# Attention's pair sums two steps behind their additions, and the scan's products with C in pairs of steps

## The chip, the cores and the metric

The kernel runs on one core of a Trainium2 chip, written in Bass with Tile. A core has five engines that work through queues of their own: PE (TensorE: matrix products, weights loaded by PEld), DVE (VectorE), ACT (ScalarE), POOL (GpSimd) and SP (SyncE, which here issues DMAs). SBUF holds 128 partitions; PSUM has 8 banks of 2 KB per partition, and products land there. The metric is the device time of one execution in microseconds, lower is better. Before the change it is 2339.04 us, the median of four runs from 2338.34 to 2341.28.

## The reference

One layer: x is 4 images of 256 channels and 32 × 32 pixels (N = 1024 tokens). A mixer with a residual is followed by a mixture of experts with a residual. The part that the change touches:

```python
def selective_scan(u, dt, Bm, Cm, A, Dp):          # per channel, 16 states
    dA = jnp.exp(dt[..., None] * A)
    dBu = (dt * u)[..., None] * Bm[:, :, None, :]
    def step(h, inp):
        dA_t, dBu_t, C_t = inp
        h = dA_t * h + dBu_t
        return (h, jnp.einsum('bds,bs->bd', h, C_t))
    ...
    return ys + u * Dp
def mamba(xs, ...):                                # 4 of them, 64 channels each, inner width 128
    u, z = jnp.split(xs @ inw.T, 2, axis=-1)
    u = silu(causal_conv(u)); xdbc = u @ xpw.T
    dt = softplus(xdbc[..., :4] @ dtw.T + dtb)
    return selective_scan(...) * silu(z) @ outw.T
def mha(x, ...):                                   # 8 heads of 32
    att = softmax(q @ k.T / hd ** 0.5)
    return (att @ v) @ outw.T + outb
...
xm = mamba_v(layernorm(xs)) + skip_scale * xc      # then gates and convolutions along the tokens
x_local = conv1d(xm2); x_global = mha(xm2)
x_out = gelu(layernorm(concat([x_local, x_global]) @ fc_w.T + fc_b))
...                                                # 3x3 convolution, layernorm, projection
```

After it come the experts: 8 of them, 256 to 1024 to 256 with gelu, the two best for each token, weighted.

## The kernel before

Every engine's queue holds its instructions in the order in which the code emits them; the scheduler moves nothing. Buffers are rotating slots of pools: `act8` (8 KB a partition, 8 slots), `act4` (4 KB, 7 slots), `act2` (2 KB, 17 slots), and `ps`, the 8 PSUM banks. An instruction that writes a slot waits until the slot's last reader is done.

*The scan.* For image b and channel quarter n (inner width 128) a tile holds 32 channels × 4 states on its partitions and half of the tokens (512) on its free axis. A part (b, n, h) is half h of the tokens; it has 16 steps i, with q, g = divmod(i, 4): block q of four states, channel group g of 32. One step is: `decay`, dA = exp(dt·A) on ACT, emitted three steps ahead (L620); `inflow`, dBu on DVE into a PSUM bank (L628); `step`, the recurrence as one DVE scan instruction (L639), then for h = 0 a POOL copy of the last column, from which h = 1 goes on (L643), and on POOL the product of the states with C (L644, `hs` by `cs`). Once a block, `sums_of` lets PE add the four states of each channel: four products with the constant `quads` into the bank `yp` (L650). `spread_b` makes the block's B with PE (`bs`, L612), `spread_c` its C by four DMAs from SP (`cs`). The function `scan` emits, in this order, step i of a part: at g = 1 `spread_b` of the next block; entries of the table `before` (the end of the part before: last sums, `gather`, `project_out`, `add_skip`); of `behind` (dt of the next part: `dtp`, softplus, two POOL products L575 and L579, `dts` by DMA); of `group` (projections of the next quarter: `project_z`, `project_u` at 9 and 10 with product `up` L528, `silu`, which reads them into u at L549, `project_c`); `spread_c` at g = 0; at g = 1 `sums_of` of the block before; then decay, inflow and step. `gather` is DVE's y (L657) and POOL's product with z (L660); `project_out` is PE's `op` (L665); `add_skip` writes `xm` on DVE (L671).

*Around it.* While image b is scanned, the convolutions of image b−1 run between the steps (`depthwise3`, products `fp`, gate g; their first product is `qd`, L802, which reads xm once the image is whole). In the middle of the image the scan stops, the attention of b−1 runs, with the three-by-three taps of b−2 (L1161) and the layernorm of b+1 (`normalised`, L472) beside it, and the scan goes on when attention is almost over; `joined` then does the fc product of b−1. After the last image come its convolutions, its attention, and 35 tiles of expert work.

*Attention.* 32 steps (g, h, kt) per image: two groups of four heads, two halves of the queries, eight tiles of 128 keys. A step emits the logits of the next step (PE `st`, four banks, L967; ACT's four exps, L977), then values times exps (PE into the values bank, L1013). Softmax's denominators: at odd kt DVE adds the four exps of kt to those of kt−1 (L1023), and at the next step, ahead of that step's other work on DVE, `sum_pair` lets PE add them over the keys (L987; the profile writes its output as `av`). Both banks, values and sums, are taken at kt = 0. A block (g, h) ends in `end_block` at the next block's kt = 1, after its adds: ACT's Ln and Exp (L995, L1000), DVE's reduce (L999) and multiply (L1003).

Of the kernel before, what the change touches and what calls it, by code (L numbers as in the profile page):

```python
# [9 lines left out]
F32 = mybir.dt.float32  # L10
AF = mybir.ActivationFunctionType
ALU = mybir.AluOpType
AX = mybir.AxisListType

P = 128
# [4 lines left out]
HALF = 512  # L20
NB, DM, DIN, DS, DTR, KC = 4, 64, 128, 16, 4, 4
NHEAD, HD = 8, 32
# [50 lines left out]
def network(  # L73
# [27 lines left out]
    nc = tc.nc  # L101
# [41 lines left out]

    with tc.tile_pool(name="w_conv", bufs=1) as wp, tc.tile_pool(
        name="act8", bufs=8
    ) as act8, tc.tile_pool(name="act4", bufs=7) as act4, tc.tile_pool(
        name="act2", bufs=17
    ) as act2, tc.tile_pool(name="steps", bufs=2) as actd, tc.tile_pool(
        name="steps4", bufs=6
    ) as acts, tc.tile_pool(name="rows", bufs=3) as actc, tc.tile_pool(  # L150
        name="small", bufs=1
    ) as small, tc.tile_pool(
        name="spread", bufs=2, space=bass.MemoryType.DRAM
# [123 lines left out]
        ones = experts.every  # L277


        GD, GS = DIN // 32, DS // 4  # L280
# [58 lines left out]
        def ps(name):  # L339

            return psum.tile([P, HALF], F32, tag="ps", name=name)
# [9 lines left out]

        def a4(name):
            return act4.tile([P, N], F32, tag="a4", name=name)

        def a2(name, rows=P):
            return act2.tile([rows, HALF], F32, tag="a2", name=name)

        def half(h):
            return ts(h, HALF)
# [3 lines left out]
        def log_exp():  # L363
            if loaded[0] != LOG_EXP:
                nc.scalar.preload_act_table_set(LOG_EXP)
                loaded[0] = LOG_EXP
# [150 lines left out]
        T = {}  # L517
# [90 lines left out]
        def spread_b(b, n, h, q):  # L608
            bs = T[b, n, h, "bs", q] = ps(f"bs_{b}_{n}_{h}_{q}")
            for i, r in enumerate(states):  # L610
                s = DTR + 4 * q + i
                nc.tensor.matmul(  # L612
                    bs[r], xpwT_s[:, n, s : s + 1].to_broadcast([P, 32]),
                    T[b, n, "u"][:, half(h)], start=True, stop=True,
                )
# [16 lines left out]
        def step(b, n, h, i):  # L632
            q, g = divmod(i, GD)
            dBu = T.pop((b, n, h, "dBu", i))
            hs = T[b, n, h, "hs", i] = a2(f"hs_{b}_{n}_{h}_{i}")
            if h == 0 and i == 0:
                T[b, n, "last"] = small.tile([P, NSTEP], F32, tag="last", name=f"last_{b}_{n}", bufs=2)
            last = T[b, n, "last"][:, i : i + 1]
            nc.vector.tensor_tensor_scan(  # L639
                hs, T[b, n, h, "dA", i], dBu, 0.0 if h == 0 else last, ALU.mult, ALU.add  # L640
            )
            if h == 0:
                nc.gpsimd.tensor_copy(last, hs[:, HALF - 1 : HALF])  # L643
            nc.gpsimd.tensor_tensor(hs, hs, T[b, n, h, "cs", q], ALU.mult)  # L644

        def sums_of(b, n, h, q):
            if q == 0:
# [19 lines left out]
        def add_skip(b, n, h):  # L667
# [7 lines left out]


        before = {
            1: [(sums_of, GS - 1)], 3: [(gather,)], 6: [(project_out,)], 8: [(add_skip,)],
        }

        behind = {
# [44 lines left out]
        def scan(at, i, stop):  # L726

            b, n, h = parts[at]
            q, g = divmod(i, GD)
            if g == 1 and q + 1 < GS:  # L730
                spread_b(b, n, h, q + 1)
            if at > 0:
                for what, *args in before.get(i, ()):
                    if parts[at - 1] not in finished:
                        what(*parts[at - 1], *args)
            if at + 1 < len(parts):
                for what, *args in behind.get(i, ()):
                    if what is not spread_b or not stop:
                        what(*parts[at + 1], *args)
            nb, nn = (b, n + 1) if n + 1 < NB else (b + 1, 0)  # L740
            if nb < B:
                for what, *args in group[h].get(i, ()):
                    what(nb, nn, *args)
            if g == 0 and q + 1 < GS:
                spread_c(b, n, h, q + 1)
            if g == 1 and q > 0:
                sums_of(b, n, h, q - 1)
            ahead = i + LEAD
            if ahead < NSTEP:
                decay(b, n, h, ahead)  # L750
            elif at + 1 < len(parts) and not stop:
                decay(*parts[at + 1], ahead - NSTEP)
            if i + 1 < NSTEP:
                inflow(b, n, h, i + 1)
            elif at + 1 < len(parts) and not stop:
                inflow(*parts[at + 1], 0)
            step(b, n, h, i)

        finished = set()
# [149 lines left out]
        NK = N // P  # L909
# [38 lines left out]
        def attention(b):  # L948

            v8, qk = QKV.pop(b)
            rows = [
                largest(b, g, qk[g][:, 0, :], qk[g][:, 1, :]) if shifted else None
                for g in range(2)
            ]
            yield 1
            steps = [(g, h, kt) for g in range(2) for h in range(2) for kt in range(NK)]

            def logits(g, h, kt):

                q, k = qk[g][:, 0, :], qk[g][:, 1, :]
                sts = [ps(f"st_{b}_{g}_{h}_{kt}_{i}") for i in range(4)]
                for i in range(4):
                    r = ts(i, HD)
                    nc.tensor.matmul(  # L967
                        sts[i], k[r, ts(kt, P)], q[r, half(h)], start=True, stop=not shifted
                    )
                    if shifted:  # L970
                        nc.tensor.matmul(
                            sts[i], ones[HD * i : HD * i + 1, :],
                            rows[g][HD * i : HD * i + 1, half(h)], start=False, stop=True,
                        )
                es = [a2(f"e_{b}_{g}_{h}_{kt}_{i}") for i in range(4)]
                for i in range(4):
                    nc.scalar.activation(es[i], sts[i], AF.Exp, scale=1.0 / HD**0.5)  # L977
                return es

            log_exp()  # L980
            ahead = logits(*steps[0])
            pairs, accs, ending = [], [None, None], []

            def sum_pair():
                kt, acc, es = pairs.pop()
                for i in range(4):
                    nc.tensor.matmul(  # L987
                        acc[ts(i, HD)], ones[:, 0:HD], es[i], start=(kt == 1), stop=(kt == NK - 1)
                    )

            def end_block(g, h, values, total):

                low, out = a2(f"low_{b}_{g}_{h}"), OT[b][g][:, half(h)]
                at = (2 * b + g) * 2 + h
                nc.scalar.activation(low, total, AF.Ln, bias=added)  # L995
                if shifted:
                    nc.scalar.activation(low, low, AF.Exp, scale=-1.0)
                else:
                    nc.vector.tensor_reduce(sums[:, 0, at : at + 1], total, AX.X, ALU.max)  # L999
                    nc.scalar.activation(  # L1000
                        low, low, AF.Exp, scale=-1.0, accum_out=sums[:, 1, at : at + 1]
                    )
                nc.vector.tensor_tensor(out, values, low, ALU.mult)  # L1003

            for at, (g, h, kt) in enumerate(steps):
                es = ahead
                if at + 1 < len(steps):
                    ahead = logits(*steps[at + 1])
                if kt == 0:

                    accs = [ps(f"av_{b}_{g}_{h}_{w}") for w in range(2)]
                for i in range(4):
                    nc.tensor.matmul(  # L1013
                        accs[0][ts(i, HD)], v8[:, kt, ts(4 * g + i, HD)], es[i],
                        start=(kt == 0), stop=(kt == NK - 1),
                    )
                if pairs:
                    sum_pair()
                if kt % 2 == 0:
                    first = es  # L1020
                else:
                    for i in range(4):
                        nc.vector.tensor_tensor(first[i], first[i], es[i], ALU.add)  # L1023
                    pairs.append((kt, accs[1], first))
                    if ending:
                        end_block(*ending.pop())
                if kt == NK - 1:
                    ending.append((g, h, *accs))
                if at == len(steps) - 3:
                    T["attended", b] = True  # L1030
                yield 1
            sum_pair()
            yield 1
            end_block(*ending.pop())
            yield 1

        def local(b):
# [317 lines left out]
        with tc.manual_schedule(engines=ALL):  # L1355
# [4 lines left out]
            for b in range(B):  # L1360
                for p in range(PARTS):
                    at = b * PARTS + p
                    stop = b > 0 and p == PARTS // 2 - 1 or at == len(parts) - 1
# [71 lines left out]
class Experts:  # L1435
# [11 lines left out]
    T = 256  # L1447
# [649 lines left out]
```

## Time and profile before

| | |
|---|---|
| median of four runs | 2339.04 us (2338.34 to 2341.28) |
| profiled execution | 2339.41 us, of which 2337.6 us are the span |
| mean granted PE clock | 0.928 |
| PE, DVE, ACT, POOL busy | 2040.3, 1608.9, 1145.3, 1111.6 us |
| L644, product with C, 512 times | 673.4 us, mean 1318 ns (1257 to 2302) |
| L643, copy of the last column, 256 times | 61.8 us, mean 241 ns |
| L639, scan, 384 rows found | 475.2 us, mean 1268 and 1207 ns |
| attention of images 0 to 3 | 472 to 571, 858 to 958, 1292 to 1392, 1730 to 1820 us |
| experts | about 1850 to 2337 us |

The profile is of one execution of the program. Times are microseconds unless marked ns. "L644" is line 644 of the kernel. In the rows of single instructions the first two columns are the start from the beginning of the span and the duration; x8 says how many instructions are drawn together; what stands in square brackets is idle time of the engine ahead of the row, and the instruction whose end was waited for. In rows of groups, the figures after the first bar are the busy time in us and the mean ns of one, after the second the idle time ahead of them and what ended it. A few per cent of the product rows are missing from the record.

### The profile page before, as it was taken

The numbers are of one execution on the slowest core, as the hardware profiler recorded it, in microseconds if no ns is written. First come the engines' busy times: TensorE is split into PE (matmuls) and PEld (weight loads), VectorE is DVE, ScalarE is ACT, GpSimd is POOL, SyncE is SP. The second block draws the span as 40 slices with busy tenths as digits, with TensorE's granted clock in tenths as the row PEclk, the third lists the DMA queues.
The fourth block names the chain that finished last, engine by engine and source line by source line (L and its number), as shares of the span: only waits on it lengthen the run. The fifth ranks groups of instructions, "written<-read, shape, count | busy, mean of one in ns | idle before, by whom it ended". The sixth has DMA issues, their size and how long they took to land. (4 is left out here: it accounts for less than half of the span.)

```text
span 2337.6 us, 28285 instructions
## 1 busy us (share of the span) xinstructions
PE 2040.3 (87%) x8810; PEld 917.0 (39%) x8810; DVE 1608.9 (69%) x2295; ACT 1145.3 (49%) x1953; POOL 1111.6 (48%) x1185
## 2 busy tenths in 40 slices
PE   7777776999976899986669999668999999999995
PEld 2122111332211232222113223205752678888884
DVE  3989998967898989789989877987355264211111
ACT  3654546468656467664264775415258432222221
POOL 0788887722787750476877115572140012422221
PEclk7987988999998999998789999768999999999997
DMA  2454443310343330133433202443340165877765
GB/s 85 122 143 111 110 107 78 81 38 29 95 103 93 83 73 28 44 102 96 120 76 74 55 1 59 104 136 117 86 139 1 43 193 171 256 196 194 195 186 156
DMA packets 155022, 244.33 MB, mean 105 GB/s; under 512 B 34212, under 2 KB 103492, under 8 KB 154856
## 3 DMA queue, kind: packets, MB, share of 16 engines
q1 hardware_dynamic: 135680, 217.07, 33.6%
q0 software_dynamic: 13264, 17.85, 4.1%
q10 hardware_dynamic: 5912, 7.45, 0.9%
q8 instruction: 74, 1.21, 0.2%
q14 instruction: 92, 0.75, 0.1%
HBM read 141.17 MB, written 33.98 MB: 75 GB/s over the span
## 5 line engine op out<-in xcount | busy, mean ns | idle before, releaser
L644 POOL TENSOR_TENSOR hs<-hs,cs 128x512 f32<-128x512 f32 x512 | 673.4, 1318 | 158.5 <-DVE hs L639 94.1
L620 ACT ACTIVATE dA<-dts,A 128x512 f32<-128x512 f32 x512 | 341.7, 713 | 196.3 <-DMA dts<-dt 118.2
L650 PE MATMUL yp<-hs,quads 128*32 128x512 f32 x1024 | 317.2, 669 | 117.3 <-POOL hs L644 77.3
L1964 POOL DMA_INDIRECT Y<-ys,dest x70 | 113.7, 1625 | 526.0 <-DVE ys L1958 519.7
L628 DVE TENSOR_TENSOR dBu<-dts,bs 128x512 f32<-128x512 f32 x384 | 260.0, 678 | 87.5 <-PE bs L612 36.2
L977 ACT ACTIVATE e<-st 128x512 f32<-128x512 f32 x512 | 263.8, 603 | 95.8 <-PE st L967 92.1
L1943 ACT ACTIVATE hs<-h,b 128x256 f32<-128x256 f32 x280 | 116.7, 472 | 358.9 <-PE h L1938 201.5
L1938 PE MATMUL h<-xT,w 128*128 128x256 f32 x1120 | 254.3, 384 | 7.3 <-DVE xT L1916 7.3
L1948 PE MATMUL y<-w,hs 128*128 128x256 f32 x1120 | 257.7, 382 | 1.7 <-ACT hs L1943 1.7
L639 DVE TENSOR_TENSOR_SCAN hs<-dA,last,dBu 128x512 f32<-128x512 f32 x192 | 243.5, 1268 | 0.3
L639 DVE TENSOR_TENSOR_SCAN hs<-dA,dBu 128x512 f32<-128x512 f32 x192 | 231.7, 1207 | 6.5 <-PE av L987 4.0
L1938 PEld LDWEIGHTS h<-xT,w 128*128 128x128 f32 x1120 | 214.5, 192 | 45.6 <-issue 8.1
L1916 DVE COPY xT<-xp 128x512 f32<-128x512 f32 x35 | 24.2, 691 | 296.2 <-PE xp L1915 296.1
L1948 PEld LDWEIGHTS y<-w,hs 128*128 128x128 f32 x1120 | 210.8, 191 | 37.9 <-issue 8.7
L612 PE MATMUL bs<-u,xpwT_s 128*32 128x512 f32 x1024 | 164.0, 679 | 67.5 <-DVE hs L639 34.4
L1023 DVE TENSOR_TENSOR e<-e,e 128x512 f32<-128x512 f32 x256 | 171.4, 731 | 61.7 <-ACT e L977 33.6
L643 POOL COPY last<-hs 128x1 f32<-128x1 f32 x256 | 61.8, 241 | 308.4 <-DVE hs L639 300.4
L650 PEld LDWEIGHTS yp<-hs,quads 128*32 128x32 f32 x1024 | 54.4, 116 | 353.1 <-POOL hs L644 220.2
L967 PE MATMUL st<-qk 32*128 32x512 f32 x1024 | 173.4, 638 | 1.3 <-DVE hs L639 1.3
L1013 PE MATMUL av<-e,v 128*32 128x512 f32 x1024 | 141.1, 610 | 0.0
L528 PE MATMUL up<-xn,inwk 64*128 64x512 f32 x256 | 132.3, 661 | 0.0
L967 PEld LDWEIGHTS st<-qk 32*128 32x128 f32 x1024 | 59.0, 183 | 115.7 <-issue 85.4
(278 smaller groups left out, 2690.4 us busy)
## 6 DMA issues: line engine op xcount, KB each, us to landing
w<-in_W_dram SPq DMA_DIRECT2D x136, 512.0 KB, 4.9
dts<-dt SPq DMA_DIRECT2D x512, 128.0 KB, 2.3
cs<-cd SPq DMA_DIRECT2D x512, 64.0 KB, 2.1
xs<-XS SPq DMA_DIRECT2D x35, 260.0 KB, 4.6
b<-in_b_dram SPq DMA_DIRECT2D x35, 128.0 KB, 4.8
xn<-in_x_dram SPq DMA_DIRECT2D x8, 512.0 KB, 6.8
XL<-xl SPq DMA_DIRECT2D x8, 512.0 KB
xl<-XL SPq DMA_DIRECT2D x4, 1024.0 KB
```

The source lines that it names most:

```text
L612: nc.tensor.matmul(bs[r], xpwT_s[:, n, s : s + 1].to_broadcast([P, 32]), T[b, n, "u"][:, half(h)], start=True, stop=True,)
L620: nc.scalar.activation(dA, T[b, n, h, "dts", g][:, 0, :], AF.Exp, scale=A[:, g, n, q : q + 1])
L628: nc.vector.tensor_tensor(dBu, T[b, n, h, "dts", g][:, 1, :], T[b, n, h, "bs", q], ALU.mult)
L639: nc.vector.tensor_tensor_scan(hs, T[b, n, h, "dA", i], dBu, 0.0 if h == 0 else last, ALU.mult, ALU.add)
L644: nc.gpsimd.tensor_tensor(hs, hs, T[b, n, h, "cs", q], ALU.mult)
L650: nc.tensor.matmul(T[b, n, h, "yp"][ts(g, 32)], quads, T[b, n, h, "hs", q * GD + g], start=(q == 0), stop=(q == GS - 1),)
L967: nc.tensor.matmul(sts[i], k[r, ts(kt, P)], q[r, half(h)], start=True, stop=not shifted)
L977: nc.scalar.activation(es[i], sts[i], AF.Exp, scale=1.0 / HD**0.5)
L1013: nc.tensor.matmul(accs[0][ts(i, HD)], v8[:, kt, ts(4 * g + i, HD)], es[i], start=(kt == 0), stop=(kt == NK - 1),)
L1023: nc.vector.tensor_tensor(first[i], first[i], es[i], ALU.add)
L1938: nc.tensor.matmul(hp[:, i, :], w1(c, k), xT[:, c, :], start=(c == 0), stop=(c == NC2 - 1))
L1948: nc.tensor.matmul(yp[:, ts(t, C)], hs[:, k, ts(t, P)], w2(k), start=(k == 0), stop=(k == NHC - 1))
```

## The change

Attention: the exps of even steps get two tiles of two heads each, in `act4`; those of odd steps stay in `act2`. `pairs` becomes a queue: at an odd step the pair of two steps before is summed, and only then are this step's adds emitted. The bank for the sums is taken at a block's first sum (its kt = 3), and `end_block` is emitted directly after its last sum, that is at kt = 1 of the next block, ahead of the adds. At the end there is one empty turn, then the last sum and the last `end_block`.

Scan: two steps share one tile in `act4`; the copy of the last columns and the product with C are emitted once for two steps, after the odd one, with C repeated over the two. `sums_of` moves from g = 1 to g = 2, and the entries of `before` each move by one step. `act4` goes from 7 to 11 slots and `act2` from 17 to 9; in bytes the two together stay as they were.

```diff
-    ) as act8, tc.tile_pool(name="act4", bufs=7) as act4, tc.tile_pool(
-        name="act2", bufs=17
+    ) as act8, tc.tile_pool(name="act4", bufs=11) as act4, tc.tile_pool(
+        name="act2", bufs=9
...
+        def pair(name):
+            return act4.tile([P, 2, HALF], F32, tag="a4", name=name)
...
-            hs = T[b, n, h, "hs", i] = a2(f"hs_{b}_{n}_{h}_{i}")
+            if i % 2 == 0:
+                T[b, n, h, "two"] = pair(f"hs_{b}_{n}_{h}_{i}")
+            two = T[b, n, h, "two"]
+            hs = T[b, n, h, "hs", i] = two[:, i % 2, :]
...
+            if i % 2 == 0:
+                return
             if h == 0:
-                nc.gpsimd.tensor_copy(last, hs[:, HALF - 1 : HALF])
-            nc.gpsimd.tensor_tensor(hs, hs, T[b, n, h, "cs", q], ALU.mult)
+                nc.gpsimd.tensor_copy(
+                    T[b, n, "last"][:, i - 1 : i + 1].rearrange("p (g a) -> p g a", a=1),
+                    two[:, :, HALF - 1 : HALF],
+                )
+            nc.gpsimd.tensor_tensor(
+                two, two,
+                T[b, n, h, "cs", q].rearrange("p (a x) -> p a x", a=1).to_broadcast([P, 2, HALF]),
+                ALU.mult,
+            )
...
-            1: [(sums_of, GS - 1)], 3: [(gather,)], 6: [(project_out,)], 8: [(add_skip,)],
+            2: [(sums_of, GS - 1)], 4: [(gather,)], 7: [(project_out,)], 9: [(add_skip,)],
...
-            if g == 1 and q > 0:
+            if g == 2 and q > 0:
                 sums_of(b, n, h, q - 1)
...
-                es = [a2(f"e_{b}_{g}_{h}_{kt}_{i}") for i in range(4)]
+                if kt % 2 == 0:
+                    two = [pair(f"e_{b}_{g}_{h}_{kt}_{i}") for i in range(2)]
+                    es = [two[i // 2][:, i % 2, :] for i in range(4)]
+                else:
+                    es = [a2(f"e_{b}_{g}_{h}_{kt}_{i}") for i in range(4)]
...
-                kt, acc, es = pairs.pop()
+                (g, h, kt), values, es = pairs.pop(0)
+                if kt == 1:
+                    sums_at[0] = ps(f"sum_{b}_{g}_{h}")
                 for i in range(4):
                     nc.tensor.matmul(
-                        acc[ts(i, HD)], ones[:, 0:HD], es[i], start=(kt == 1), stop=(kt == NK - 1)
+                        sums_at[0][ts(i, HD)], ones[:, 0:HD], es[i],
+                        start=(kt == 1), stop=(kt == NK - 1),
                     )
+                if kt == NK - 1:
+                    end_block(g, h, values, sums_at[0])
...
-                if pairs:
-                    sum_pair()
                 if kt % 2 == 0:
                     first = es
                 else:
+                    if pairs:
+                        sum_pair()
                     for i in range(4):
                         nc.vector.tensor_tensor(first[i], first[i], es[i], ALU.add)
-                    pairs.append((kt, accs[1], first))
-                    if ending:
-                        end_block(*ending.pop())
-                if kt == NK - 1:
-                    ending.append((g, h, *accs))
+                    pairs.append(((g, h, kt), values, first))
...
-            sum_pair()
             yield 1
-            end_block(*ending.pop())
+            sum_pair()
             yield 1
```

More of the change, by code (lines that the diff above doesn't have):

```diff
@@ L981, in attention @@
             ahead = logits(*steps[0])
-            pairs, accs, ending = [], [None, None], []
+            pairs, sums_at = [], [None]
             def sum_pair():
-                kt, acc, es = pairs.pop()
+                (g, h, kt), values, es = pairs.pop(0)
+                if kt == 1:
+                    sums_at[0] = ps(f"sum_{b}_{g}_{h}")
                 for i in range(4):
                     nc.tensor.matmul(
-                        acc[ts(i, HD)], ones[:, 0:HD], es[i], start=(kt == 1), stop=(kt == NK - 1)
-                    )
+                        sums_at[0][ts(i, HD)], ones[:, 0:HD], es[i],
+                        start=(kt == 1), stop=(kt == NK - 1),
+                    )
+                if kt == NK - 1:
+                    end_block(g, h, values, sums_at[0])
             def end_block(g, h, values, total):
@@ L1009, in attention @@
                 if kt == 0:
-                    accs = [ps(f"av_{b}_{g}_{h}_{w}") for w in range(2)]
+                    values = ps(f"av_{b}_{g}_{h}")
                 for i in range(4):
                     nc.tensor.matmul(
-                        accs[0][ts(i, HD)], v8[:, kt, ts(4 * g + i, HD)], es[i],
+                        values[ts(i, HD)], v8[:, kt, ts(4 * g + i, HD)], es[i],
                         start=(kt == 0), stop=(kt == NK - 1),
                     )
-                if pairs:
-                    sum_pair()
                 if kt % 2 == 0:
@@ L1031, in attention @@
                 yield 1
+            yield 1
             sum_pair()
-            yield 1
-            end_block(*ending.pop())
             yield 1
```

## The prediction

> **What bounds the kernel now.** I read the page's head first, then busy time by stretch, then PE's waits, then the rows of single instructions on either side of the change.
>
> ```profile
> span 2337.6 us, 28285 instructions
> ...
> PE 2040.3 (87%) x8810; PEld 917.0 (39%) x8810; DVE 1608.9 (69%) x2295; ACT 1145.3 (49%) x1953; POOL 1111.6 (48%) x1185
> ```
>
> The shares are averages over unlike stages, so the stretches decide (columns: PE, PEld, DVE, ACT, POOL busy with instruction counts, PE's granted clock, DMA share, GB/s):
>
> ```profile
> 200.00:345.00 145.00, 113.69 (x382) 24.98 (x378) 144.73 (x165) 77.71 (x117) 124.54 (x135) 0.94 0.43 106
> ...
> 472.00:571.00 99.00, 98.58 (x653) 28.66 (x652) 64.00 (x84) 76.34 (x149) 16.87 (x14) 1.00 0.10 31
> ...
> 1850.00:2337.00 487.00, 453.54 (x2131) 389.65 (x2129) 135.98 (x384) 124.21 (x271) 116.76 (x125) 0.97 0.67 188
> ```
>
> A scan stretch (first row) is DVE's: 144.73 of 145 us, with POOL at 86%. An attention stretch (second) is PE's: 98.58 of 99. The experts at the end (third) are PE's too and are not touched, so 1850 to 2337 moves as one block. PE's waits show the place of the scan's edit (us in total, times, longest):
>
> ```profile
> PEld yp L650 <- POOL hs L644: 220.2, 156, 3.5
> ...
> PE yp L650 <- POOL hs L644: 77.3, 93, 2.6
> ```
>
> PE stands at the state sums because POOL's product is late. Most of it costs nothing, since DVE, not PE, bounds the scan. It costs where PE work queued behind the sums is what DVE will need: at each change of channel group the second `up` (L528, 3.70 us) is queued behind them, and its u, its dA and the next scan hang on it. DVE's rows there:
>
> ```profile
> 439.42 0.69 DVE L628 TENSOR_TENSOR dBu<-dts,bs 128x512 f32<-128x512 f32 x1 [2.24 <-ACT u L549]
> 442.08 1.22 DVE L639 TENSOR_TENSOR_SCAN hs<-dA,bs 128x512 f32<-128x512 f32 x1 [1.97 <-ACT dA L620]
> ```
>
> **Attention, cost by cost.** A pair of steps in the steady state, and a pair under the image convolution's taps:
>
> ```profile
> 541.56 1.04 PE L987 MATMUL av<-e,every 128*32 128x512 f32 x8
> 542.54 1.14 PE L967 MATMUL st<-qk 32*128 32x512 f32 x8
> 543.61 1.06 PE L1013 MATMUL av<-e,v 128*32 128x512 f32 x8
> 544.60 1.35 PE L967 MATMUL st<-qk 32*128 32x512 f32 x8
> 545.88 1.06 PE L1013 MATMUL av<-e,v 128*32 128x512 f32 x8
> ...
> 927.91 1.07 PE L1013 MATMUL av<-e,v 128*32 128x512 f32 x8
> 928.79 2.83 PE L987 MATMUL av<-e,every 128*32 128x512 f32 x8
> ```
>
> From 541.56 to 546.76 is 5.20 us of PE for two steps, with no gap: four logits and values groups and one group of pair sums, 0.98 start to start. ACT's eight exps (L977) take about 4.1 of that and DVE's four adds (L1023) 2.5, so both have slack. In the steady state the adds end about 2.4 us before their sum is reached, and queueing the sum a step later buys nothing: instructions removed on PE, none; added, none.
>
> Under the taps (898 to 936 in the second attention) DVE works 7.0 us a pair and the adds end late: the sums take 2.03, 2.35, 2.85 with 0.99 idle ahead, and 2.83 us instead of 0.98, which is 7.1 us lost. The sum now comes one step, about 2.6 us, later. While DVE is saturated a fixed delay is won once, not per pair, so I take 2.6 us for each of the two attentions that have taps (the second and third; the first and last have no L1161 row in their stretch): −5.2 (ends 0 and −14.2).
>
> Each of an attention's three inner block boundaries shows an `st` group of 1.84 instead of 1.35 us (1755.75, 1777.04, 1798.33), because a block's two accumulators are taken together at its first step while the old pair waits for the end of its block. Now the sum's bank is taken only at kt = 3, so there is one bank more for logits when it happens. 12 × 0.49 = −5.9 (ends 0 and −5.9).
>
> Against this: at kt = 1 the adds stand on DVE behind the block's reduce and multiply (L999, L1003, 0.69 each), which wait for ACT's Ln and Exp. What queues behind the adds is the sum of step 3; they get ready just as PE reaches it. 0 to 0.2 us at 16 blocks, taken as +1.0 of 3.2. The pair tiles of the even steps now come from the 4 KB pool, which in the last attention is shared with the expert tiles: their Y scatter (L1964, 1.6 us each) must end before about ten exps can write; 0 to +4, I take 0 since PE has queued work of earlier steps. Sum −10; ends −20 and +7.
>
> **Scan, POOL's part.** Removed: 256 products of 512 elements (1.27 us in the undisturbed rows, 1.22 start to start) with 128 copies (0.18, 0.26 start to start). Added: no instruction, but 256 products become 1024 wide. No row has that. Nearest below: `xl` (L505), also a 128x1024 product on POOL; nearest above: `xm` (L834):
>
> ```profile
> L834 POOL TENSOR_TENSOR xm<-g,xm 128x1024 f32<-128x1024 f32 x8 | 25.1, 3148 | 22.6 <-ACT g L826 22.6
> ...
> L505 POOL TENSOR_TENSOR xl<-xn,r 128x1024 f32<-128x1024 f32 x6 | 12.0, 2002 | 13.9 <-ACT r L372 13.9
> ```
>
> Ends 2.00 and 3.15; twice 1.27 less one fixed part gives 2.4, between them and near the quieter row, and I take that. A first-half part (16 steps) costs DVE 16 × 1.72 + 2 × 0.65 (y and xm) = 28.8 us, and POOL then 8 × (0.26 + 2.4) + 3 × 1.27 (two dt, one y) = 25.1: POOL keeps behind DVE, and the saved 8 × 0.26 is time POOL had free. Worth 0 by itself; cover lost at p = (28.8 − 3.8)/8 − 0.26 = 2.87 us.
>
> The Trainium skill, "GPSIMD Engine Reference", in its reconciliation with measured numbers gives a tensor_tensor add of 2048 elements as 4497 ns and about 2.6 cycles an element, so that the elements and not the fixed part make the time. With this trace's 1272 ns for 512 that is an estimate of 1.272 + 512 × (4497 − 1272)/1536 = 2.35 us for a pair; by the L505 row it is 2.00. By either the sum is unchanged.
>
> **Scan, PE's part.** A block's last product ends about 1.13 us later (2.4 for two instead of 1.27 for one); its sums are queued one step, 1.72 us, later. PE's wait at a block falls by some 0.6 us, worth nothing where DVE is full. What is worth something: at i = 10 the second `up` is now emitted ahead of the sums instead of behind. With the sums' 1.0 us and their wait out of its way, up, u and dA come 1.0 to 1.9 us earlier at the group changes (the lines at 439 and 442; the same picture at 151, 826, 1259 and 1424) and at three image starts, where the same `up` took 7.19 us (336.35; granted clock 0.86 in 300 to 350). 5 × 1.0 + 3 × 1.5 = 9.5 at most; DVE meets another wait (ACT g, PE bs) within 8 us at the image starts, so I take −6 (ends −9.5, +5.1).
>
> The end +5.1: gather, project_out and add_skip come one step later each (DVE y and xm, PE op, POOL y; none of these issues a DMA, and SP's order of cs and dts is as before). add_skip now stands directly ahead of qd (L802), which reads xm. xm ran at 337.81 and qd at 345.18 behind `up`, so 1.7 us later is hidden; with `up` shorter it would show: 3 × 1.7.
>
> The same page family, "TensorE: Matmul & The Clock Gate", Part 1, says that the array falls to half rate after an idle window of about 3.4 us. The row it bears on is `up` at 7.19 us right after a wait of 3.48 for DVE's hs, against 3.70 elsewhere; it would speak against bunching the sums, and by it one more such halving would cost 3.5 us. No row tells whether a gap crosses that line now.
>
> Together −16: the profiled execution, 2339.4 (1.8 of it outside the span; 0.4 above the median of the four runs), becomes 2323.4, the median 2323.
>
> **Rivals.**
> *Everything is hidden* (15%). DVE fills 144.73 of 145 in the scan, PE 98.58 of 99 in attention; if the logits wait for banks anyway and the group change ends on ACT, ±3 remain: 2338. For it: adds ready 2.4 us early in the steady state. Against: the 7.1 us under the taps and the 2.24 + 1.97 on DVE are really idle.
>
> *POOL becomes the bound of the first halves* (13%). Place: products against copies and dt in h = 0. Above 2.87 us a pair, POOL falls behind in each of 16 parts; at L834's 3.15 a part takes 8 × 3.41 + 3.8 = 31.1, so +2.3 × 16 = +36: 2375. For it: single products stretched to 2.18 beside DVE's 128x1024 operations (384.91). Against: those are few, and L644's mean is 1318 against a minimum of 1257.
>
> *The pools pinch* (12%). act2 falls from 17 to 9; a dA may now have to wait for the scan five before it instead of seven. If each of 32 parts stands once for a dA (0.71 us, L620's mean): +23, less half the gains: 2354. Against: dA is queued three ahead, the scan it waits for is two further back.
>
> *More is won* (10%). If the 77.3 us of PE waits at L650 also freed the fc and fp products that hold up DVE's bs (36.2 us of dBu waits), a third of those and all taps loss go: −16 − 12 − 9 = 2302.
>
> **Numbers.** My case 50%, at 2313 to 2334 by itself. A measurement here tells 0.2%, 4.7 us, from nothing. Faster: 50 + 10 = 60; within: 15; slower: 13 + 12 = 25. 2308 leaves out about 7% below, 2358 about 11% above.
>
> **What would show it.** Right: L644 with 256 rows of 2.2 to 2.6 us; POOL below 86% in 200 to 345; no L987 above 1.5 us in the first attention and fewer than four in the second; `st` after a block's end at 1.35; DVE's wait for u at the group change near 1. Wrong: L644 above 2.87 with DVE waiting for POOL; exps waiting for DVE e or for the Y scatter; qd waiting for DVE xm; attention stretches no shorter than 99, 100, 100 and 90 us.

## The result and the profile after

The changed kernel takes 2343.93 us (median of 38 runs, 2337.06 to 2352.1) against 2339.26 us for the kernel before (61 runs, 2334.89 to 2342.48). The ratio is 1.0023 with a 95% interval of 1.0018 to 1.0028: about 5 us slower, where 16 us less had been forecast.

The head of the page of the changed kernel:

```profile
span 2342.0 us, 27820 instructions
...
PE 2004.8 (86%) x8810; PEld 905.2 (39%) x8810; DVE 1622.7 (69%) x2295; ACT 1148.0 (49%) x1953; POOL 1032.6 (44%) x801
```

POOL has 384 instructions and 79 us less. DVE has the same 2295 instructions, and 13.8 us more of busy time; nothing in the forecast said so. The same stretches as before (PE, PEld, DVE, ACT, POOL busy, granted clock, DMA share, GB/s):

```profile
200.00:345.00 145.00, 105.91 (x391) 23.09 (x383) 144.71 (x165) 76.40 (x115) 113.37 (x76) 0.88 0.42 106
472.00:571.00 99.00, 97.71 (x637) 28.02 (x630) 60.02 (x83) 74.71 (x146) 17.29 (x11) 0.98 0.08 27
```

DVE still bounds the scan and PE still bounds attention. POOL went from 86% to 78% of the scan stretch. The product with C, by form (busy us, mean ns of one, idle ahead), and PE's waits for it:

```profile
L655 POOL TENSOR_TENSOR hs<-hs,cs 128x1024 f32<-128x1024 f32 x256 | 615.0, 2404 | 190.2 <-DVE hs L645 115.8 <-PE rp L381 10.8 <-DMA dts<-dt 9.2
```

```profile
PEld yp L665 <- POOL hs L655: 194.3, 83, 6.1
...
PE yp L665 <- POOL hs L655: 105.4, 59, 5.2
```

A pair takes 2.40 us, as forecast. PE's wait for the products at the sums, weight loads and products of PE added, is 299.7 us instead of 297.5, in 142 places instead of 249: as much waiting in fewer, longer pieces. DVE at the group change that the prediction showed:

```profile
437.01 0.70 DVE L631 TENSOR_TENSOR dBu<-dts,bs 128x512 f32<-128x512 f32 x1 [2.53 <-PE bs L615]
438.81 1.22 DVE L645 TENSOR_TENSOR_SCAN hs<-dA,bs 128x512 f32<-128x512 f32 x1 [1.10 <-ACT dA L623]
```

3.63 us idle instead of 4.21: something is won there. Laying the two traces scan by scan on each other, the first quarters (n = 0) of images 1, 2 and 3 end 2.5, 2.7 and 2.8 us better than they began. The rest of the trace gives it away again.

**Where DVE's 14 us are.** They are in operations of DVE on SBUF alone, those with two inputs above all, and copies and operations with one number per partition; dBu and the recurrence, which read PSUM, keep their durations (346.5 and 346.7 us for dBu in the two traces). One of them beside POOL, in the kernel before:

```profile
1084.46 1.26 POOL L644 TENSOR_TENSOR hs<-hs,cs 128x512 f32<-128x512 f32 x1 [0.44 <-DVE hs L639]
...
1084.53 1.27 DVE L1631 TENSOR_TENSOR lg<-lg,bg_s 128x64 f32<-128x64 f32 x1
```

and in the changed kernel:

```profile
1086.83 2.34 POOL L655 TENSOR_TENSOR hs<-hs,cs 128x1024 f32<-128x1024 f32 x1 [0.98 <-DVE lg L1647]
...
1086.85 2.40 DVE L1650 TENSOR_TENSOR lg<-lg,bg_s 128x64 f32<-128x64 f32 x1
```

The DVE operation needs about 0.22 us by itself (its shortest row). It starts just after POOL's product and ends 0.08 us after it, in both kernels: it has stood through the whole of POOL's instruction. Twice the instruction, twice the wait. Larger operations run after it: a 128x512 addition that began inside a product ended 0.55 us behind it, one of 128x1024 1.08 us. Summed over the trace, the DVE operations that began while such a product ran, and were over 0.15 us longer than the shortest row of their kind in any trace, lost 26.0 us before (30 operations), 40.4 in the changed kernel (34) and 27.0 with single products (32, in e2 below). That is where the 14 us lie. Not everything on SBUF alone is held up: a batch-norm statistic that began inside a product at 1064.55 took its usual 0.39 us. Two of the larger operations (mean ns), before and after:

```profile
L411 DVE SCALAR_TENSOR_TENSOR d<-xl,V,d 128x1024 f32<-128x1024 f32 x16 | 25.1, 1566 | 0.4 <-ACT d L406 0.3
L507 DVE TENSOR_TENSOR xn<-xn,r 128x1024 f32<-128x1024 f32 x6 | 8.6, 1440 | 3.5 <-POOL xl L505 3.5
```

```profile
L414 DVE SCALAR_TENSOR_TENSOR d<-xl,V,d 128x1024 f32<-128x1024 f32 x16 | 26.3, 1642 | 0.6 <-ACT d L409 0.5
L510 DVE TENSOR_TENSOR xn<-xn,r 128x1024 f32<-128x1024 f32 x6 | 11.5, 1924 | 4.4 <-POOL xl L508 4.4
```

The Trainium skill, "SBUF — State Buffer", in the section on the two separate sides, states this as a rule: the port pair that DVE and GpSimd share is locked exclusively, for a whole instruction, and the other engine stands meanwhile; on DVE's side it names the instructions with two inputs in SBUF and those in a two-port mode. The rows above agree. The prediction did not use it; by it, longer products cost DVE time wherever DVE has such operations.

**Attention.** DVE's waits at a block's end, before and after (us in total, times, longest):

```profile
DVE sums L999 <- ACT low L995: 23.4, 11, 3.9
```

```profile
DVE sums L1023 <- ACT low L1019: 69.2, 11, 10.0
```

The reduce of end_block now stands on DVE's queue as soon as the additions of kt = 7 are issued, while the sums that it needs are queued two steps later on PE. The first block boundary of the second attention, before:

```profile
890.61 0.69 DVE L999 TENSOR_REDUCE sums<-av 128x1 f32<-128x512 f32 x1 [2.03 <-ACT low L995]
```

and in the changed kernel:

```profile
888.89 1.04 PE L1008 MATMUL sum<-e,every 128*32 128x512 f32 x8
...
890.79 0.69 DVE L1023 TENSOR_REDUCE sums<-sum 128x1 f32<-128x512 f32 x1 [5.73 <-ACT low L1019]
...
892.15 2.49 DVE L1047 TENSOR_TENSOR e<-e,e 128x512 f32<-128x512 f32 x4
...
894.23 1.52 PE L1008 MATMUL sum<-e,every 128*32 128x512 f32 x8
```

DVE idles 5.73 us instead of 2.03, the additions of kt = 1 come late behind it, and the sum that reads them takes 1.52 us where an undisturbed one (888.89) takes 1.04. From the first to the last logits the four attentions take 3.1, 0.1, 0.2 and 1.6 us longer than before, 5.0 together. Under the taps something is won: two sums of 2.83 us remain in the second attention, where four of 2.03 to 2.85 us had stood. The attention as a whole is no shorter for it.

### The profile page after: what moved, and what is told of

It reads as the page before. It is cut to its first block, busy times and chain, and to the rows that moved or that the text cites. A ratio compares the mean times of both kernels' runs of the same rounds, so it can differ in the third digit from the quotient of the medians.

```text
span 2342.0 us, 27820 instructions
## 1 busy us (share of the span) xinstructions
PE 2004.8 (86%) x8810; PEld 905.2 (39%) x8810; DVE 1622.7 (69%) x2295; ACT 1148.0 (49%) x1953; POOL 1032.6 (44%) x801
## 5 line engine op out<-in xcount | busy, mean ns | idle before, releaser
L655 POOL TENSOR_TENSOR hs<-hs,cs 128x1024 f32<-128x1024 f32 x256 | 615.0, 2404 | 190.2 <-DVE hs L645 115.8
L665 PE MATMUL yp<-hs,quads 128*32 128x512 f32 x1024 | 244.3, 705 | 142.7 <-POOL hs L655 105.4
L615 PE MATMUL bs<-u,xpwT_s 128*32 128x512 f32 x1024 | 174.6, 698 | 47.9 <-DVE hs L645 34.7
L651 POOL COPY last<-hs 128x2 f32<-128x2 f32 x128 | 32.9, 257 | 358.3 <-DVE hs L645 347.9
L665 PEld LDWEIGHTS yp<-hs,quads 128*32 128x32 f32 x1024 | 36.2, 117 | 319.3 <-POOL hs L655 194.3
```

Source lines behind the costliest of these rows:

```text
L615: nc.tensor.matmul(bs[r], xpwT_s[:, n, s : s + 1].to_broadcast([P, 32]), T[b, n, "u"][:, half(h)], start=True, stop=True,)
L655: nc.gpsimd.tensor_tensor(two, two, T[b, n, h, "cs", q].rearrange("p (a x) -> p a x", a=1).to_broadcast([P, 2, HALF]), ALU.mult,)
L665: nc.tensor.matmul(T[b, n, h, "yp"][ts(g, 32)], quads, T[b, n, h, "hs", q * GD + g], start=(q == 0), stop=(q == GS - 1),)
```

## The experiments

Each ratio is to the kernel before, run on the same chip beside it: one chip for e1 to e4, a second for e5 to e9, a third from e10 on. So ratios are compared between experiments, and a difference of ratios is turned into us by 2339 us. Two theories stood at the start. The *port theory*: the long POOL products hold up DVE. The *queue theory*: the end of a block stands ahead of the additions on DVE's queue.

**e1_layout: tiles and pools alone.** Against the changed kernel (`...` stands for what is left out of the lines):

```diff
-            if i % 2 == 0:
-                return
             if h == 0:
-                nc.gpsimd.tensor_copy(T[b, n, "last"][:, i - 1 : i + 1]..., two[:, :, HALF - 1 : HALF])
-            nc.gpsimd.tensor_tensor(two, two, ...to_broadcast([P, 2, HALF]), ALU.mult)
+                nc.gpsimd.tensor_copy(last, hs[:, HALF - 1 : HALF])
+            nc.gpsimd.tensor_tensor(hs, hs, T[b, n, h, "cs", q], ALU.mult)
...
-            if g == 2 and q > 0:
+            if g == 1 and q > 0:
```

The entries of `before` go back too, and attention's loop is that of the kernel before.

> Kept of the change: the pool sizes and the tiles for two (states and even-step exps in the 4 KB pool). Undone: products in pairs, the later state sums, the order in attention. If the pools pinch, most of the 4.7 us are here already: 2342 to 2345. If the loss lies in the long POOL products holding up DVE (port theory) or in the block's end standing ahead of the additions on DVE (queue theory), this is the kernel before in other slots: 2337.5 to 2341.

Measured: 2329.1 us, 0.9948 (0.9929 to 0.9966). Neither theory had this: the tiles and pools alone win 12 us. The changed kernel therefore loses not 5 but 17 us against its own layout.

**e2_no_pairs: the changed kernel with single products** (the diff above as far as its first line of `...`, alone).

> The changed kernel with single products and copies; all else as changed. Port theory: DVE's 128x1024 operations with two SBUF inputs and the small router operations fall back to the durations before (DVE busy from 1622.7 to about 1608), and of those 14 us some half lay in stretches that DVE bounds: 2336 to 2340. Queue theory: unchanged, 2342.5 to 2345, since attention has hardly a state product.

Measured: 2330.86 us, 0.9962 (0.9946 to 0.9978). The port theory's direction holds, with more than its size: the pairs cost 0.0061 of the time, 14 us, where 4 to 8 had been expected. DVE busy is 1607.6 us.

**e3_scan_only: the changed scan, attention as before.**

> The changed scan (pairs and later state sums) with attention in the order of before. Queue theory: attention's loss is gone, the gain at the image starts stays: 2333 to 2337. Port theory: the scan's loss is all here, the gain under the taps is gone: 2341 to 2345.

Measured: 2338.56 us, 0.9984 (0.9970 to 0.9998). Between the two expectations: 9 us better than the changed kernel, so attention's order costs too, but 8 us worse than the layout, so the scan holds a loss as well. Both theories have a share.

**e4_adds_first: the changed kernel with the additions ahead of end_block.**

```diff
                 if kt == NK - 1:
-                    end_block(g, h, values, sums_at[0])
+                    ending.append((g, h, values, sums_at[0]))
...
                     pairs.append(((g, h, kt), values, first))
+                    if ending:
+                        end_block(*ending.pop())
...
             sum_pair()
+            end_block(*ending.pop())
             yield 1
```

> The changed kernel, but at kt = 1 the four additions are emitted ahead of end_block. Queue theory: DVE's wait of the block-end reduce for ACT falls from 69 to about 25 us; 0.5 us at 12 sums and about 3 us in each of the first three attentions come back: 2333 to 2338. Port theory: attention was not the place, 2342 to 2344.

Measured: 2346.72 us, 1.0019 (1.0002 to 1.0036). DVE's wait fell from 69.2 to 22.3 us, as the queue theory says, and in the profiled execution the four attentions took about 1 us less than before instead of 5 more. That execution, 2338.91 us, is 7.8 us faster than the median; the median did not move beyond its interval (1.0019 against 1.0023). A miss for the queue theory as far as it stood alone.

**e5_late_singles: as late as the pair, half as long.**

```diff
-            nc.gpsimd.tensor_tensor(two, two, ...to_broadcast([P, 2, HALF]), ALU.mult)
+            for j in range(2):
+                nc.gpsimd.tensor_tensor(two[:, j, :], two[:, j, :], T[b, n, h, "cs", q], ALU.mult)
```

> The changed kernel, but each pair's product is two POOL instructions of 512 elements one after the other, still after the odd scan: as late as the pair, half as long. Port theory (a DVE operation with two SBUF inputs stands until POOL's running instruction ends): DVE's busy time falls from 1623 to about 1608 and the time to that of single products, some 0.995 to 0.999 of before. If lateness of the products was the cost: DVE busy may fall, the time stays at 1.001 to 1.003 of before.

Measured: 2329.26 us, 0.9954 (0.9936 to 0.9972). The same POOL work in the same places, cut in two, is 0.0069 or 16 us faster than the change, and as fast as single products after each scan. What costs is the length of the instruction and not its lateness. DVE's busy time fell to 1614.5 us, not to the expected 1608. From the first scan to the start of the last block's four scans the trace divides so (us; the last column is the time in it during which PE had half its clock):

| kernel | stretch | DVE busy | DVE idle | PE at half clock |
|---|---|---|---|---|
| before | 1499.9 | 1310.5 | 189.4 | 251 |
| changed | 1502.0 | 1324.6 | 177.5 | 365 |
| e1_layout | 1487.3 | 1307.6 | 179.7 | 249 |
| e2_no_pairs | 1481.6 | 1309.4 | 172.2 | 294 |
| e5_late_singles | 1487.5 | 1316.2 | 171.2 | 263 |
| e6_layout_late_sums | 1481.7 | 1312.7 | 169.0 | 284 |
| e3_scan_only | 1494.8 | 1326.9 | 167.9 | 345 |
| e8_layout_pairs | 1530.9 | 1322.3 | 208.6 | 401 |

Each row is one execution; that of e1 is 4.5 us above the median of its runs, that of e8 5.6 above, that of e2 6.1 below, and the others lie within 1.5. Every kernel of the table with pairs has 1322 to 1327 us of DVE work, every one without 1308 to 1316. The change won 12 us of DVE's idle time and lost 14 by making its work longer.

DVE's work is not the whole of the cost. Of the 14.5 us by which e5's stretch is shorter than the changed kernel's, 8.4 are DVE's work and 6.3 its idle time. PE's wait for the products is not behind that: it is longer in e5, 319.7 us against 299.7. PE's half-clock time is shorter by 102 us, and what part of the 6.3 us comes by the clock no run separates.

**e6_layout_late_sums and e8_layout_pairs: the two halves of the scan's change apart** (e6: single products with the sums at g = 2; e8: pairs with the sums at g = 1; attention as before in both).

> Of the change: tiles and pool sizes, and the state sums at a block's third step; single products, attention as before. If the later sums are worth what the trace shows at the image starts (3 us each, and 1 us at group changes): 0.990 to 0.994 of before. If they are worth nothing: as the layout alone, 0.993 to 0.997.

> Of the change: tiles and pool sizes, and the products in pairs; state sums early, attention as before. Port theory: DVE busy about 1623, 8 to 14 us over the layout alone: 0.998 to 1.002 of before; the sums at g = 1 now wait for a product that ends 1.1 us later, which may add some us. If pairs are harmless: 0.993 to 0.997.

Measured: e6 2323.93 us, 0.9935 (0.9920 to 0.9951); e8 2365.1 us, 1.0096 (1.0082 to 1.0111). The later sums alone are worth 3 us over the layout, which is inside the two intervals; 0.9935 lies in both expected ranges, so e6 does not decide between them. Pairs with early sums cost 35 us, far beyond the expectation. With early sums the second `up` is behind sums that wait for a pair, and PE's wait for the products grows from 270 us in e1 to 371. Where e8 loses, PE and then DVE:

```profile
230.46 7.19 PE L531 MATMUL up<-xn,inwk 64*128 64x512 f32 x8
237.58 1.93 PE L665 MATMUL yp<-hs,quads 128*32 128x512 f32 x8
239.44 7.19 PE L531 MATMUL up<-xn,inwk 64*128 64x512 f32 x8
```

```profile
248.57 0.69 DVE L631 TENSOR_TENSOR dBu<-dts,bs 128x512 f32<-128x512 f32 x1 [6.63 <-PE bs L615]
250.37 1.22 DVE L645 TENSOR_TENSOR_SCAN hs<-dA,bs 128x512 f32<-128x512 f32 x1 [1.11 <-ACT dA L623]
```

Both `up` groups run at half clock (7.19 against 3.70 us), and DVE stands 7.7 us where the layout alone has no gap. In the whole trace 70 of 256 `up` products take over 800 ns, 29 in e1. The later sums are what makes the pairs bearable: they take 26 us of those 35 back (0.9984 in e3 against 1.0096).

**e9_before_other_banks and e10_spare_bank: where the layout's 12 us come from.** In e1's trace the gain begins at the first step of image 1, where bs (L612) no longer waits for a scan. Which PSUM bank a tile gets is decided when the kernel is built, from what is free, and the layout had changed it. e9 adds one small product into a bank ahead of the scan; e10 adds one where it matters:

```diff
+            if b > 0 and n == 0 and h == 0 and i == 8:
+                spare = ps(f"spare_{b}_{n}_{h}_{i}")
+                nc.tensor.matmul(spare[0:32, 0:32], quads, quads, start=True, stop=True)
             ahead = i + LEAD
```

> The kernel before with one added product of 32 x 32 into a spare PSUM bank ahead of the scan; its result is not used. It shifts which bank the later products get (1451 of 1679 tiles differ); nothing else changes. If the layout's gain of 12 us comes from the tiles and slots, this is the kernel before: 0.999 to 1.001. If it comes from the rotation of banks, this moves too, to either side, by 3 us or more.

> The kernel before with one added product of 32 x 32 (result not used) at a block's third step in the first part of images 1 to 3. It takes the PSUM bank that bs (L612) of the last block would have taken, so that this bs no longer waits for the scan two steps back; three waits of PE on DVE go, nothing else of the order changes. If the layout's gain is the succession of banks at the image starts (bs at 334.49 waited 3.48 us, the layout's at 331.68 did not): 0.995 to 0.998 of before. If the gain lies in the SBUF slots: 0.9995 to 1.0005.

Measured: e9 2339.47 us, 0.9999 (0.9990 to 1.0008); e10 2327.86 us, 0.9953 (0.9940 to 0.9966). By its expectation e9 spoke for the slots, but its trace shows that it did not test the question: the banks have other numbers, and bs at the start of image 1 still waits 3.48 us for the scan. e10 adds its product at three places and wins 11 us, as much as the layout won. Before, such a wait stood at two of the three, at the starts of images 1 (3.48 us) and 2 (4.74 us); from the first scan of quarter n = 0 to the first of the next these two became 6.2 and 6.9 us shorter, and image 3's did not (93.5 and 93.9 us). The kernel before, and e10, at the start of image 1:

```profile
334.49 1.93 PE L612 MATMUL bs<-u,xpwT_s 128*32 128x512 f32 x8 [3.48 <-DVE hs L639]
336.35 7.19 PE L528 MATMUL up<-xn,inwk 64*128 64x512 f32 x8
```

```profile
329.66 0.25 PE L750 MATMUL spare<-quads 128*32 128x32 f32 x2
329.97 1.06 PE L612 MATMUL bs<-u,xpwT_s 128*32 128x512 f32 x8
330.96 3.70 PE L528 MATMUL up<-xn,inwk 64*128 64x512 f32 x8
```

Without the wait of 3.48 us PE keeps its full clock, so `up` is both earlier and half as long, and quarter n = 0 of image 1 takes 78.8 us instead of 85.0. That e1 wins by the same cause is likely and not shown: in its trace these two places gain 4.7 and 3.8 us, and a further 7 us are gained in the quarters n = 2 of images 1 to 3, where e10 gains nothing in sum. The rule that the prediction weighed, of the Trainium skill's "TensorE: Matmul & The Clock Gate", Part 1, agrees with this pair of rows. The wait just ahead is not all that counts, though: in e10's image 3 `up` took 7.19 us (at 1144.77) with no wait directly before it, after waits of 2.49 and 2.84 us some products earlier.

**e11_adds_first_no_pairs and e12_attention_only: attention's part.** e11 is e2 with the edit of e4; e12 is e1 with attention's new order.

> The changed kernel with single products, and with end_block after the additions. Against single products alone (0.996 of before): if end_block ahead of the additions costs attention what its trace shows (5 us over the four attentions), 0.993 to 0.995. If the cost of the new attention is elsewhere: 0.9955 to 0.997.

> Of the change: tiles and pool sizes, and attention's new order; single products, state sums as before. Against the layout alone (0.995): if attention's order loses 6 to 9 us, 0.997 to 0.999; if it wins what was forecast (10 us), 0.990 to 0.992.

Measured: e11 2322.88 us, 0.9932 (0.9919 to 0.9945), with e6 the fastest of all; e12 2326.59 us, 0.9949 (0.9936 to 0.9962), between its two expected ranges. On the early-sums layout the new attention is worth nothing either way (0.9949 against 0.9948). On the late-sums layout it costs 0.0027 (e2 against e6; the intervals overlap), and with the additions ahead of end_block this is gone: 0.9932 against 0.9935. DVE's wait at the block's end, in e2 and in e11:

```profile
DVE sums L1014 <- ACT low L1010: 67.5, 11, 8.4
```

```profile
DVE sums L1014 <- ACT low L1010: 22.3, 11, 3.1
```

**e13_change_again.**

> The changed kernel itself beside the other three on one chip: 1.001 to 1.003 of before.

Measured: 2343.77 us, 1.0025 (1.0009 to 1.0041). The loss is there again, on the chip on which e10 to e12 won.

## Why the prediction was wrong, by its own steps

The total, in ratios put one on the other: tiles and pools −0.0052 (e1), later sums −0.0013 (e6), attention's new order +0.0027 (e2), pairs +0.0061 (to the changed kernel's 1.0023). In us: −12, −3, +6 and +14. The shares hold for this order alone: added ahead of attention's new order the pairs cost 0.0049 (e3 against e6), and attention's order then 0.0039.

- *Scan, POOL's part: "Worth 0 by itself; cover lost at p = 2.87 us".* This is the step that failed. The price of a pair was right, 2.40 us, and POOL never became the bound. The cover was wrong: the only thing asked of POOL's instruction was whether POOL keeps up, not whom it keeps from working while it runs. The sign was in the rows of before, where DVE's 128x64 addition took 1.27 us beside a product of 1.26, and where the prediction itself quoted a POOL product of 2.18 us beside a DVE operation and read it as POOL's loss alone. 14 us of DVE work came of it between the first and the last scan, where the prediction had called DVE the bound, and the kernel lost 14 to 16 us by the pairs (e2, e5).
- *Scan, PE's part: −6, ends −9.5 and +5.1.* The sign is right, and the places: image starts and group changes are faster. One reading was wrong: `up` took 7.19 us at two of the three image starts, not at all three; in image 3 it took 3.70 (1154.78). By itself the move measures −3 us. Beside pairs it is worth 26, because pairs with early sums would have cost 35; the estimate that PE's wait at a block falls by 0.6 us "worth nothing where DVE is full" did not see that PE, with fewer and longer waits, runs more of its products at half clock (365 us of the stretch instead of 251).
- *The clock rule, left out of the sum.* "No row tells whether a gap crosses that line now": e8 and e10 bear on it. Two waits of 3.48 and 4.74 us, removed, are worth 11 us in all, and e8 loses where `up` runs at half clock.
- *Attention: −10, ends −20 and +7.* Measured 0 to +9 (e12 against e1; the changed kernel against e3). The 5.9 us of banks did not come: the `st` group of 1.84 us is still there at 886.23, one step earlier. The hazard of the additions behind end_block was named but priced at the waiting sum alone, 1.0 us; on DVE the wait grew by 46 us over the attentions. What part of attention's loss comes by that wait stays open, since e4, which takes most of that wait away, is not faster.
- *Pools.* Taken as 0, with a rival in which they pinch. The layout won 12 us, most likely by a side effect: another succession of PSUM banks. The wait at stake, 3.48 us, stands in the prediction, but no row of before showed that the tiles in SBUF decide about it. A pinch was seen in one execution: in e1's last attention eight exps stood 5.19 us, and that attention took 9 us longer.
- *The rivals.* "POOL becomes the bound" did not come, nor did "everything is hidden". The slower side came by a mechanism that none of them had.

What stays open: why the additions ahead of end_block win about 7 us without pairs (e11 against e2) and none that could be measured with them (e4). The spread of single runs there, 2336 to 2360 us, is larger than the effect.

## What to carry to other kernels

Before merging two POOL instructions into one, list the DVE operations in the same stretches that read two tiles of SBUF, and copies and products within SBUF, and charge each with the longer instruction: fewer and longer is worse for the neighbour, whatever it saves on POOL. An operation moved to another place of an in-order queue must be priced on every engine that holds a part of it; end_block's reduce was cheap on PE's side and blocked DVE. And compare a changed kernel with its own layout too, because slots that are handed out when the kernel is built can hide a loss of 17 us behind a gain of 12.

## What the runs showed of the hardware

- A small DVE addition, copy or scalar operation on SBUF that begins inside a POOL product ends with it: 1.27 us beside 1.26, 2.40 beside 2.34, for 0.22 us of work. Larger ones run behind it. The recurrence and the operations with a PSUM operand did not change, nor did batch-norm statistics on SBUF (0.39 us inside a product of 2.38).
- An elementwise product on POOL with one operand repeated over two halves took 2.36 us undisturbed for 1024 elements, more than the 2.00 us of the product `xl` of the same size without the repetition, and less than two single ones (2.54). That the repetition makes the difference is not shown.
- PE's `up` group takes 3.70 us at full clock and 7.19 at half clock, and a wait of 3.48 us just ahead of it was enough for the slower. Half-clock time over the stretch of the table was 251 us before and 365 us in the changed kernel.
- More half-clock time is not by itself slower: e11, the fastest kernel, has 313 us of it over the same stretch. At e10's two places the full clock, and `up` earlier by it, came with quarters 6.2 and 6.9 us shorter.
